# Residual additions of a two-block attention kernel: by VectorE, or by accumulating transfers

## The chip, the core and the metric

The kernel runs on one core of a Trainium2 chip. Its engines are TensorE (PE in the profile; PEld is its weight load), VectorE (DVE), ScalarE (ACT), GpSimd (POOL) and SyncE (SP), which only issues transfers. Each engine executes its own instructions in a fixed order and waits on semaphores for the others. Transfers are issued from an engine's queue and carried out by 16 DMA engines. The metric is device time of one execution in microseconds; lower is better.

## The reference

Eight images of 512 channels by 1024 positions (float32) go through two attention blocks. Cut to what matters:

```python
# layer 0: 32 groups, 8 heads
h = group_norm(x, gn_weight, gn_bias)
q, k, v = split(w_qkv @ h + b_qkv)              # per head, 64 channels
a = softmax(q.T @ k * scale) @ v                # per head
x = x + (w_proj @ a + b_proj)                   # first residual
# layer 1: 8 groups, one head of 512 channels
h = group_norm(x, gamma, beta)
q, k, v = q_w @ h + q_b, k_w @ h + k_b, v_w @ h + v_b
a = softmax(q.T @ k * scale) @ v
return x + (p_w @ a + p_b)                      # second residual
```

The two lines with `x +` are the subject of this study.

## The kernel before

**Tiles.** A channel tile is 128 channels by 1024 positions; an image has four (`KC`). Results are written in halves of 128x512 (`HT` = 512), so that an image has eight half tiles of 256 KB.

**Products.** Matrix products are Strassen–Winograd products. `wino` makes a product of 2x2 blocks with seven block products, taken in the order 1, then a `middle`, then 4 and 3. They accumulate in three kinds of PSUM banks: a (products 1, 2), b (6, 7, 4) and c (5, 3), two of each (i = 0, 1). When a block of the result is complete, `wino` calls `done(i, row, c, ps, u)`, where `ps` is the bank and `u` an intermediate in SBUF (or nothing for the first block). Block (0,0) is complete after product 2, (1,1) after product 7, (1,0) after 4 and (0,1) after 3. The last two products, 4 and 3, are put off (`tail`) and run behind product 1 of the next stage, so that TensorE has work while the other engines empty the banks. `conv2` nests the scheme twice for the convolutions q, k, v and g; some of its additions run on GpSimd (L537), as do the differences that make its inner factors (`inner_factors`, L416).

**Stages.** The loop goes over the images b. Each turn has: layer 0's attention of image b; `projection`, the last convolution of layer 0, of image b; the g convolution and layer 1 of image b-1 (`layer1_scores`, `layer1_rest`); and the v, k and q convolutions of image b+1. So layer 1 of image j ends beside the v convolution of image j+2. While that happens, four "ahead" loads (L209) bring the image after that one, and VectorE takes its statistics (`half_stats`, L98) as background. Image 6's layer 1 has the g convolution of image 7 beside it, and image 7's layer 1 comes at the very end.

**The first residual.** Before the projection, SP loads the four tiles of x (L1062). For each completed block, VectorE adds bank, bias and x into the x tile (L938), then the intermediate u (L942 or L944), and then takes the statistics of the result for layer 1. Its four tiles are stored to a DRAM buffer, `spills[b]`.

**The second residual.** Layer 1 of image b loads `spills[b]` again (`load_again`, L1020). `values1` makes the last product (`av`). For each completed block, VectorE multiplies by the reciprocal sums r into a temporary o (L757, or L759 and L760), adds bias and x into the x tile (L762), and SP stores that half to the output (L763). The factors of this product, `sz`, are sums and differences of z, made by VectorE (L159 to L162) just before and during its first products.

**Order.** A tile scheduler puts the instructions of each engine in an order by priorities and readiness. Only instructions wrapped in `tc.keep_in_program_order` keep the order of the program, all matmuls among them. So TensorE's order is written out by hand, and most of the other engines' order is the scheduler's.

Of the kernel before, what the change touches and what calls it, by code (L numbers as in the profile page):

```python
# [9 lines left out]
F32 = mybir.dt.float32  # L10
I32 = mybir.dt.int32
AF = mybir.ActivationFunctionType
ALU = mybir.AluOpType
# [16 lines left out]
def two_attention_blocks_kernel(  # L30
# [145 lines left out]
    def main_path(ctx):  # L176
# [30 lines left out]
        def load_x(b, c, what):  # L207
            t = big_tile(f"{what}_{b}_{c}")
            nc.sync.dma_start(t, x[b, c * P : (c + 1) * P, :])  # L209
            return t  # L210
# [130 lines left out]
        def weight(n):  # L341
            return weight_factors(weight_part(n))
# [400 lines left out]
            )  # L743
            return total, {p: [x[:, i, :] for x in fs[p] for i in range(2)] for p in fs}

        def values1(b, zf, ef, r, xt, uid, hooks):
            def mm(p, i, ps, start):
                for k in range(4):
                    matmul(
                        ps, zf[p][k // 2][:, k % 2, ts(i, P)], ef[p][k], start=start and k == 0, stop=k == 3, skip_group_check=True  # L750
                    )

            def done(i, row, c, ps, u):
                oc = 2 * row + i
                o = upool.tile([P, HT], F32, tag="o", bufs=2, name=f"o_{uid}_{oc}_{c}")
                if u is None:
                    nc.vector.tensor_mul(o, ps, r[:, c, :])  # L757
                else:
                    nc.vector.tensor_add(o, ps, u)  # L759
                    nc.vector.tensor_mul(o, o, r[:, c, :])  # L760
                xh = xt[oc][:, ts(c, HT)]
                nc.vector.scalar_tensor_tensor(xh, o, obias[1][:, oc : oc + 1], xh, ALU.add, ALU.add)  # L762
                nc.sync.dma_start(out[b, oc * P : (oc + 1) * P, ts(c, HT)], xh)  # L763

            wino(f"av_{uid}", mm, done, middle=(2, 5, 6, 7), hooks=hooks, back=4)
# [125 lines left out]
        def load_again(b, c, what):  # L891
            t = big_tile(f"{what}_{b}_{c}")
            nc.sync.dma_start(t, spills[b][c])
            return t
# [33 lines left out]
        def projection(b, af, xt, hooks=()):  # L928

            norm = GroupNorm(1, f"1_{b}", pinned=b > 0)  # L930
            stats, rest = [], []

            def residual(i, r, c, ps, u):
                oc = 2 * r + i
                xh = xt[oc][:, ts(c, HT)]

                tc.keep_in_program_order(
                    nc.vector.scalar_tensor_tensor(xh, ps, obias[0][:, oc : oc + 1], xh, ALU.add, ALU.add)  # L938
                )
                if (r, c) == (1, 1):  # L940

                    rest.append(lambda: tc.keep_in_program_order(nc.vector.tensor_add(xh, xh, u)))  # L942
                elif u is not None:
                    nc.vector.tensor_add(xh, xh, u)  # L944
                stats.append(lambda: norm.half_stats(oc, c, xh))

                if c == 1 - r:
                    stats.append(lambda: norm.end_stats(oc))

            def add_rest():  # L950
                for f in rest:
                    f()

            def store():
                spills[b] = spool.tile([KC, P, T], F32, tag="spill", name=f"spill_{b}")
                for c in range(KC):
                    nc.sync.dma_start(spills[b][c], xt[c])

            by_channel(
                weight("p"), af, f"p_{b}", residual, middle=(5, 6, 7, 2), hooks=[[], [], hooks, [], [add_rest]],  # L960
                after=[load_weight, store],
            )
            return norm, stats
# [43 lines left out]
        def layer1_rest(b, inner, gf, gsteps, stats, hooks, ahead):  # L1007
            first = query_factors(gf[1], f"1_1_{b}")
            total, ef = scores1(inner, gf, gsteps, first, f"1_{b}", stats)
            state = {}  # L1010

            def sums():
                state["r"] = reciprocals(total, f"1_{b}", True)

            z = by_token(
                weight("z"), hf, f"z1_{b}", hooks=[*hooks, [sums]], back=3,
                after=[load_weight, lambda: background.extend(zsteps)],
            )
            all_background()
            xt = [load_again(b, c, "x") for c in range(KC)]  # L1020
            stiles = [big_tile(f"sz{i}_{b}", (P, 2, 2, C // 2)) for i in (1, 2, 4)]
            halves = lambda t: (t[:, :, : C // 2], t[:, :, C // 2 :])
            zf, zsteps = left_sums(
                [halves(t) for t in z[:2]], [halves(t) for t in z[2:]],
                [lambda j, t=t: t[:, j, :, :] for t in stiles], nc.vector.tensor_add, nc.vector.tensor_sub,
            )
            values1(b, zf, ef, state["r"], xt, f"1_{b}", ahead)

        for b in range(B):
            extra = [[] for _ in range(2 * 2 * KC)]  # L1030
            for i, fs in enumerate(later):
                extra[i] += fs
            later = []
            h, loads, applies = [], [], []
            if b > 0:
                h, loads, applies = begun(load_again, norm1, b - 1, "h1")
            elif B > 1:
                h, loads, applies = begun(load_x, norm0, 1, "h0")
            for f in loads:
                f()  # L1040
            for i, f in enumerate(applies):
                extra[2 * i + 1].append(f)
            a = channel_tiles(f"a0_{b}")

            here = lambda *t: tc.keep_in_program_order(nc.vector.tensor_sub(*t))
            af, steps = image_factors(a, f"a_{b}", here)

            if b > 0:
                hf, t = image_factors(h, f"h1_{b - 1}", here)
                for i, fs in enumerate((t[:1], t[1:2], (t[2], t[4]), (t[6], t[3]), (t[5], t[7]), steps[:2], steps[2:4])):  # L1050
                    extra[2 * i + 3] += fs
            elif B > 1:
                hf, t = image_factors(h, "h0_1", here)
                for i, fs in enumerate((t[:2], (t[2], t[4]), (t[6], t[3]), (t[5], t[7], *steps[:2]), steps[2:4])):
                    extra[2 * i + 7] += fs
            psum_pools(f"attention_{b}", 1)
            scaled = attention0(b, q, k, v, a, extra)
            if B > 1:
                for f in steps[4:7]:
                    f()  # L1060
            psum_pools(f"products_{b}", 2)
            xt = [load_x(b, c, "x") for c in range(KC)]  # L1062
            if B > 1:

                inner, sums2 = inner_factors(hf, f"h1_{b - 1}" if b > 0 else "h0_1", tc.keep_in_program_order)
                for f in sums2:
                    f()
                norm1, stats = projection(b, af, xt, [scaled, steps[7]])
            if b > 0:
                gf, gsteps = layer1_scores(b - 1, inner)  # L1070
                _, _, mean, affine = norm_hooks(norm1, f"1_{b}")
                if b + 1 < B:
                    h, loads, applies = begun(load_x, norm0, b + 1, "h0")
                    ahead, made = factors_ahead(h, loads, applies, f"h0_{b + 1}")
                else:
                    h, loads, applies = begun(load_again, norm1, b, "h1")
                    ahead = [loads, *([f] for f in applies)]
                layer1_rest(b - 1, inner, gf, gsteps, stats, [[], mean, [], affine], ahead)
                if b + 1 < B:
                    v, norm0 = values(b + 1, made["inner"])  # L1080
                    q, k = keys_and_queries(b + 1, made["inner"], norm0, ())
            elif B > 1:
                v, norm0 = values(1, inner)
                hooks = norm_hooks(norm1, "1_0")
                hooks[0].append(lambda: background.extend(stats))
                q, k = keys_and_queries(1, inner, norm0, hooks)
            else:
                for f in (*steps[:7], scaled, steps[7]):
                    f()
                all_background()  # L1090
                norm1, stats = projection(0, af, xt)
                finish()
                background.extend(stats)
                for f in sum(norm_hooks(norm1, "1_0"), []):
                    f()
                h, loads, applies = begun(load_again, norm1, 0, "h1")
                for f in loads + applies:
                    f()
# [202 lines left out]
```

## Time and profile before

| what | value |
| --- | --- |
| median of 3 runs | 2832.25 us (2831.9 to 2833.12) |
| profiled execution | 2831.03 us; its span 2829.2 us, granted clock 0.999 |
| TensorE waiting | about 9 us in all, 3.7 of them for the first weights |
| adds of the first residual, L938 / L942 / L944 | 64 of 0.74 us / 16 of 1.17 us / the rest 0.67 to 1.13 us |
| adds of the second residual, L762 | 64 of 0.75 us |
| x tiles loaded for the first residual / the second | 32 / 32, 512 KB each |
| transfers | q1 (SP) 28.3% of 16 engines' time, q10 (ScalarE) 0.3%; none in a GpSimd queue |
| SP's issue of one transfer, L763 | 0.33 us |

A row of the timeline reads: start in us, duration in us, engine, line, operation, output<-inputs, shape, and in brackets how long the engine had stood idle before it and for whom. Consecutive equal rows may be gathered ("x8"). A row of the waits names the waiting instruction and, behind the arrow, what it waited for.

### The profile page before, as it was taken

To read this page: it belongs to the slowest core of one execution; us is meant where nothing else is said; L and a number is where in the kernel's file an instruction comes from. 1 tells how busy PE (TensorE), PEld (TensorE's weight loads), DVE (VectorE), ACT (ScalarE), POOL (GpSimd) and SP (SyncE) were. 2 spreads that over 40 slices of the span, in tenths; PEclk is the share of its full clock that TensorE was granted. 3 is DMA by queue.
4 is the path that set the end of the run, shared out by engine and by line. 5 is a ranking of instruction groups with operands and counts; after the bars stand their busy time and mean duration, and the time that the engine had idled before them with its cause. 6 is when DMAs were issued, how large, how long until landed. Compare 5 with 4: busy or idle time off the path is not lost.

```text
span 2829.2 us, 33980 instructions
## 1 busy us (share of the span) xinstructions
PE 2811.2 (99%) x12434; PEld 1691.7 (60%) x12434; DVE 2119.0 (75%) x2877; ACT 942.7 (33%) x1205; POOL 1250.6 (44%) x1249
## 2 busy tenths in 40 slices
PE   9999999999999999999999999999999999999998
PEld 5435635866367653677537674376843868338584
DVE  5588687766877778777787667877678776887765
ACT  1252452214522145221552215422154312633130
POOL 2214215842267421674117731277223772147672
PEclk9999999999999999999999999999999999999999
DMA  8634403043031330323212232123311224112301
GB/s 286 210 114 147 151 19 121 26 178 138 20 139 53 146 129 23 131 99 119 110 49 105 101 141 90 49 102 123 139 70 49 102 112 158 35 53 95 119 5 68
DMA packets 98850, 291.68 MB, mean 103 GB/s; under 512 B 10803, under 2 KB 42867, under 8 KB 88950
## 3 DMA queue, kind: packets, MB, share of 16 engines
q1 hardware_dynamic: 96886, 287.16, 28.3%
q10 hardware_dynamic: 1792, 2.29, 0.3%
q8 instruction: 100, 1.64, 0.2%
q14 instruction: 72, 0.59, 0.1%
HBM read 236.94 MB, written 52.47 MB: 102 GB/s over the span
## 4 chain that ended last, share of the span: by engine, by line
PE 97%; DVE 1%; issue 1%; POOL 0%; ACT 0%; DVEq 0%; POOLq 0%
PE sc L67 16%; PE av L67 16%; PE psb_av L67 6%; PE psb L67 5%; PE psa_av L67 4%; PE psc_av L67 4%; PE psc L67 3%; PE psa L67 3%; PE psb_z L67 3%; PE psb_p L67 3%; PE psb_k L67 3%; PE psb_g L67 3%; PE psb_v L67 3%; PE psb_q L67 2%; PE psa_p L67 2%; PE psa_z L67 2%
## 5 line engine op out<-in xcount | busy, mean ns | idle before, releaser
L639 DVE TENSOR_TENSOR sum<-sum,e 128x1024 f32<-128x1024 f32 x384 | 518.9, 1351 | 40.7 <-ACT e L635 0.9
L635 ACT ACTIVATE e<-sc 128x1024 f32<-128x1024 f32 x512 | 476.0, 1054 | 79.1 <-PE sc L67 79.1
L67 PE MATMUL sc<-q,k 64*128 64x512 f32 x2048 | 456.8, 596 | 0.0
L67 PE MATMUL av<-e,v 128*64 128x512 f32 x2048 | 453.6, 595 | 0.0
L67 PEld LDWEIGHTS sc<-q,k 64*128 64x128 f32 x2048 | 191.6, 186 | 238.5 <-ACT e L635 109.2
L67 PEld LDWEIGHTS av<-e,v 128*64 128x64 f32 x2048 | 141.4, 137 | 304.3 <-issue 304.3
L601 POOL TENSOR_TENSOR all_recs<-all_recs,rc 128x256 f32<-128x256 f32 x72 | 63.8, 887 | 541.3 <-DVE rc L599 541.3
L658 POOL TENSOR_TENSOR a<-a,r 128x512 f32<-128x512 f32 x56 | 114.9, 2051 | 261.7 <-DMA r<-rows 245.5
L599 DVE RECIPROCAL rc<-sums 128x256 f32<-128x256 f32 x72 | 126.5, 1756 | 46.7 <-PE sums L67 25.3
L653 ACT COPY a<-av 128x512 f32<-128x512 f32 x64 | 37.4, 585 | 321.9 <-PE av L67 321.9
L637 DVE TENSOR_TENSOR sum<-e,e 128x1024 f32<-128x1024 f32 x64 | 78.8, 1231 | 57.0 <-ACT e L635 57.0
L67 PE MATMUL psb<-inner,inner_h 128*128 128x256 f32 x448 | 116.1, 382 | 0.8
L67 PE MATMUL psa_av<-e,z 128*128 128x512 f32 x256 | 113.3, 595 | 0.0
L416 POOL TENSOR_TENSOR inner_h<-h,inner_h 128x256 f32<-128x256 f32 x120 | 107.5, 897 | 3.4
L140 ACT ACTIVATE h<-h,b,s 128x1024 f32<-128x1024 f32 x62 | 78.5, 1270 | 88.0 <-DMA h<-in_x 70.4
L67 PEld LDWEIGHTS psb<-inner,inner_h 128*128 128x128 f32 x448 | 83.9, 190 | 16.6 <-POOL inner L431 3.5
L464 ACT COPY psb_v<-psa_v 128x512 f32<-128x512 f32 (+1 forms) x28 | 14.5, 517 | 227.0 <-DVE o L759 144.6
L416 POOL TENSOR_TENSOR inner_h<-h 128x256 f32<-128x256 f32 x60 | 55.6, 926 | 77.4 <-ACT h L140 77.4
L699 POOL TENSOR_TENSOR sum<-sum,e 128x1024 f32<-128x1024 f32 x32 | 76.1, 2378 | 27.1 <-ACT e L695 25.9
L67 PE MATMUL psb_g<-inner_h,w_m 128*128 128x256 f32 x336 | 85.9, 383 | 0.3
L685 DVE TENSOR_TENSOR e<-psc,u 128x512 f32<-128x512 f32 x56 | 38.7, 691 | 59.0 <-PE psc L67 58.6
L537 POOL TENSOR_TENSOR v<-v,v 128x256 f32<-128x256 f32 x28 | 20.0, 726 | 141.8 <-DVE u_v L532 141.8
(361 smaller groups left out, 5749.6 us busy)
## 6 DMA issues: line engine op xcount, KB each, us to landing
x<-in_x SPq DMA_DIRECT2D x36, 512.0 KB
h<-in_x SPq DMA_DIRECT2D x32, 512.0 KB
spill<-x SPq DMA_DIRECT2D x32, 512.0 KB
h<-spill SPq DMA_DIRECT2D x32, 512.0 KB
x<-spill SPq DMA_DIRECT2D x32, 512.0 KB
out<-x SPq DMA_DIRECT2D x64, 256.0 KB
w_p<-sums_p SPq DMA_DIRECT2D x8, 1792.0 KB
r<-rows SPq DMA_DIRECT2D x112, 128.0 KB
```

What stands on the lines that cost most here:

```text
L67: tc.keep_in_program_order(nc.tensor.matmul(*args, **kw))
L140: tc.keep_in_program_order(nc.scalar.activation(dst, src, AF.Identity, bias=b, scale=s))
L416: pin(nc.gpsimd.tensor_tensor(dst, x, y, ALU.subtract))
L599: nc.vector.reciprocal(rc, sums)
L601: nc.gpsimd.tensor_tensor(all_recs, all_recs, rc, ALU.add)
L635: nc.scalar.activation(e, sc, AF.Exp, scale=(C // 8) ** -0.5)
L637: nc.vector.tensor_add(total, es[0], e)
L639: nc.vector.tensor_add(total, total, e)
L653: nc.scalar.copy(dst, av)
L658: nc.gpsimd.tensor_tensor(dst, dst, r, ALU.mult)
L685: nc.vector.tensor_add(dst[0], ps, x[0])
L699: on = lambda dst, x, y: lambda: tc.keep_in_program_order(nc.gpsimd.tensor_tensor(dst, x, y, ALU.add))
```

## The change

The result tiles no longer begin as loaded x. The results are written to SBUF with their bias, and then the residual is added to them there by a transfer from DRAM with `accum_op=add`, which reads the tile's half, adds and writes it back. These transfers are issued from GpSimd's queue, one for each half tile of 256 KB.

- First residual, all images: no load of x. Block (0,0) leaves PSUM on ScalarE with the bias; the others leave on VectorE as bank + bias + u in one operation (`biased`). Then the accumulating transfer of x's half follows. The statistics and the store to `spills[b]` come behind it, and so wait for it. The put-off addition of block (1,1) (`add_rest`) is gone.
- Second residual, images 0 to 6: no load from the spill. The multiplied result goes to a tile y, ScalarE adds the bias in place, an accumulating transfer adds the spill's half, and SP stores the half as before. Image 7's layer 1 stays as it was.

In all there are 64 + 56 = 120 accumulating transfers; 32 + 28 loads of 512 KB are gone.

```diff
 def values1(b, zf, ef, r, xt, before, uid, hooks):
     def done(i, row, c, ps, u):
         oc = 2 * row + i
-        o = upool.tile([P, HT], F32, tag="o", ...)
+        if before is None:
+            o = upool.tile([P, HT], F32, tag="o", ...)
+        else:
+            o = xt[oc][:, ts(c, HT)]
         if u is None:
             nc.vector.tensor_mul(o, ps, r[:, c, :])
         else:
             nc.vector.tensor_add(o, ps, u)
             nc.vector.tensor_mul(o, o, r[:, c, :])
+        if before is not None:
+            nc.scalar.activation(o, o, AF.Identity, bias=obias[1][:, oc : oc + 1])
+            nc.gpsimd.dma_start(o, before[oc][:, ts(c, HT)], accum_op=ALU.add)
+            nc.sync.dma_start(out[b, oc * P : (oc + 1) * P, ts(c, HT)], o)
+            return
...
 def projection(b, af, xt, hooks=()):
+    place = biased(xt, obias[0])
     def residual(i, r, c, ps, u):
         oc = 2 * r + i
+        place(i, r, c, ps, u)
         xh = xt[oc][:, ts(c, HT)]
-        tc.keep_in_program_order(
-            nc.vector.scalar_tensor_tensor(xh, ps, obias[0][:, oc : oc + 1], xh, ALU.add, ALU.add)
-        )
-        if (r, c) == (1, 1):
-            rest.append(lambda: tc.keep_in_program_order(nc.vector.tensor_add(xh, xh, u)))
-        elif u is not None:
-            nc.vector.tensor_add(xh, xh, u)
+        nc.gpsimd.dma_start(xh, x[b, oc * P : (oc + 1) * P, ts(c, HT)], accum_op=ALU.add)
         stats.append(lambda: norm.half_stats(oc, c, xh))
...
-    ..., hooks=[[], [], hooks, [], [add_rest]],
+    ..., hooks=[[], [], hooks],
...
 def layer1_rest(...):
-    xt = [load_again(b, c, "x") for c in range(KC)]
+    before = spills[b] if b + 1 < B else None
+    xt = channel_tiles(f"y_{b}") if b + 1 < B else [load_again(b, c, "x") for c in range(KC)]
...
-    values1(b, zf, ef, state["r"], xt, f"1_{b}", ahead)
+    values1(b, zf, ef, state["r"], xt, before, f"1_{b}", ahead)
...
 for b in range(B):
-    xt = [load_x(b, c, "x") for c in range(KC)]
+    xt = channel_tiles(f"x1_{b}")
```

`biased`, which was there already, is the placing function:

```python
def biased(out, bias):
    def done(i, r, c, ps, u):
        oc = 2 * r + i
        dst = out[oc][:, ts(c, HT)]
        if u is None:
            nc.scalar.activation(dst, ps, AF.Identity, bias=bias[:, oc : oc + 1])
        else:
            nc.vector.scalar_tensor_tensor(dst, ps, bias[:, oc : oc + 1], u, ALU.add, ALU.add)
    return done
```

More of the change, by code (lines that the diff above doesn't have):

```diff
@@ L744, in scores1, with values1 @@
             return total, {p: [x[:, i, :] for x in fs[p] for i in range(2)] for p in fs}
-        def values1(b, zf, ef, r, xt, uid, hooks):
+        def values1(b, zf, ef, r, xt, before, uid, hooks):
             def mm(p, i, ps, start):
@@ L754, in done @@
                 oc = 2 * row + i
-                o = upool.tile([P, HT], F32, tag="o", bufs=2, name=f"o_{uid}_{oc}_{c}")
+                if before is None:
+                    o = upool.tile([P, HT], F32, tag="o", bufs=2, name=f"o_{uid}_{oc}_{c}")
+                else:
+                    o = xt[oc][:, ts(c, HT)]
                 if u is None:
@@ L930, in projection @@
             norm = GroupNorm(1, f"1_{b}", pinned=b > 0)
-            stats, rest = [], []
+            stats = []
+            place = biased(xt, obias[0])
             def residual(i, r, c, ps, u):
                 oc = 2 * r + i
+                place(i, r, c, ps, u)
                 xh = xt[oc][:, ts(c, HT)]
-                tc.keep_in_program_order(
-                    nc.vector.scalar_tensor_tensor(xh, ps, obias[0][:, oc : oc + 1], xh, ALU.add, ALU.add)
-                )
-                if (r, c) == (1, 1):
-                    rest.append(lambda: tc.keep_in_program_order(nc.vector.tensor_add(xh, xh, u)))
-                elif u is not None:
-                    nc.vector.tensor_add(xh, xh, u)
+                nc.gpsimd.dma_start(xh, x[b, oc * P : (oc + 1) * P, ts(c, HT)], accum_op=ALU.add)
                 stats.append(lambda: norm.half_stats(oc, c, xh))
@@ L948, in residual @@
                     stats.append(lambda: norm.end_stats(oc))
-            def add_rest():
-                for f in rest:
-                    f()
             def store():
@@ L959, in projection @@
             by_channel(
-                weight("p"), af, f"p_{b}", residual, middle=(5, 6, 7, 2), hooks=[[], [], hooks, [], [add_rest]],
+                weight("p"), af, f"p_{b}", residual, middle=(5, 6, 7, 2), hooks=[[], [], hooks],
                 after=[load_weight, store],
```

## The prediction

> **What bounds the kernel.** First the page: busy shares, the granted clock, the chain that ended last.
>
> ```profile
> span 2829.2 us, 33980 instructions
> PE 2811.2 (99%) x12434; PEld 1691.7 (60%) x12434; DVE 2119.0 (75%) x2877; ACT 942.7 (33%) x1205; POOL 1250.6 (44%) x1249
> PEclk9999999999999999999999999999999999999999
> PE 97%; DVE 1%; issue 1%; POOL 0%; ACT 0%; DVEq 0%; POOLq 0%
> ```
>
> TensorE computes 99% of the span at full clock. Work taken off any other engine is worth only what TensorE waits for it. Next, therefore, TensorE's waits.
>
> ```profile
> PE tr_wk L70 <- DMA rawk<-in_w: 3.7, 1, 3.7
> PE psb_v L67 <- ACT u_v L454: 1.2, 1, 1.2
> PE psa_v L67 <- POOL h L142: 0.8, 1, 0.8
> PE psc_v L67 <- DVE x L938: 0.6, 1, 0.6
> ```
>
> These columns are total, times and longest, in us. With five lines of 0.4 to 0.5 the list sums to about 9 us. The residual's loads (36 + 28 of 512 KB) appear in no line, and the residual's vector work appears only as image 0's 0.6, with 1.2 + 0.5 just behind it. So at most 2.3 us can be gained. What decides is whether the change makes new waits. So the third step is the order of instructions of the built changed kernel, engine by engine, laid on the timeline of before. TensorE's order is the same in both.
>
> **Part 1: removed and moved work.** Per projection VectorE loses 8 operations (16 L938/L942/L944 rows of 0.7 to 1.1 us become 6 adds out of PSUM plus 2 on ScalarE); per layer-1 image 0 to 6 it loses 8 L762 rows of 0.75. That is about 11 us an image of work beside TensorE: nothing for the end, except image 0's 2.3 us at the most. The 60 loads leave SP, which nobody waits for: nothing. ScalarE gains 8 in-place biases (0.72 each, row L544) per layer-1 image, at 33% busy; they are priced where somebody is behind them. New are 120 accumulating transfers of 256 KB in GpSimd's queue. They cost d of GpSimd's time each to issue, and land a time l later; before has no such row. For d the lowest neighbours are SP's own issue (0.33 us, L209) and ScalarE's (0.56); the highest is GpSimd's 128x512 multiply (L658, 2.05). GpSimd's own L128 (a power of 128x4 numbers) takes 1.02 us, nearly all of it without data to move, as an issue is; of these rows it is the nearest in kind. I take d = 1.0. For l: a 512 KB load took 3.6 us from its issue to its first reader (shown below). Half the bytes, but they are read, added and written, so the ends are 2 and 4; I take l = 3.
>
> **Part 2: a sum that slips behind a product.** Image 1's layer 1, VectorE, before, and TensorE below it:
>
> ```profile
> 917.70 0.69 DVE L757 TENSOR_TENSOR o<-psa_av,r 128x512 f32<-128x512 f32 x1 [2.14 <-PE psa_av L67]
> 918.31 0.68 DVE L159 TENSOR_TENSOR sz<-z,z 128x512 f32<-128x512 f32 x1
> ...
> 921.37 0.69 DVE L757 TENSOR_TENSOR o<-psa_av,r 128x512 f32<-128x512 f32 x1
> ```
>
> ```profile
> 917.50 3.60 PE L67 MATMUL psa_av<-e,z 128*128 128x512 f32 x8
> 920.93 3.60 PE L67 MATMUL psc_av<-t,sz 128*128 128x512 f32 x8
> ```
>
> Product 5 (psc_av) multiplies by sz and starts the moment product 2 (psa_av) ends. Both sz sums stand ahead of the second o in before. In the changed order the first operations are y_0, y_1, and only then the two sz: y_1 waits for the end of product 2, so sz can't start sooner. TensorE then waits 0.2 (start after the product's end, as at 917.70) + 0.61 (the pitch of y_1 to the next operation) + 0.68 (first sz) + 0.1 = 1.6 us. The order is alike in all seven changed layer-1 images: 7 x 1.6 = **11.2 us**. This is the surest term.
>
> **Part 3: the statistics ahead are queued behind the new transfers.** While TensorE runs image 1's last products and the next v convolution, the loads "ahead" of a later image are issued by SP and their statistics run on VectorE. Here is before: SP, VectorE, GpSimd and TensorE.
>
> ```profile
> 934.89 5.65 SPq L209 DMA_DIRECT2D ahead<-in_x  x3
> ```
>
> ```profile
> 938.52 0.69 DVE L98 BATCH_NORM_STATS2 bnst<-ahead 128x6 f32<-128x512 f32 x1 [2.96 <-DMA ahead<-in_x]
> ```
>
> ```profile
> 946.33 1.85 POOL L416 TENSOR_TENSOR inner_h<-t_h,inner_h 128x256 f32<-128x256 f32 x2
> 969.86 0.73 POOL L537 TENSOR_TENSOR v<-v,v 128x256 f32<-128x256 f32 x1 [21.68 <-DVE u_v L532]
> ```
>
> ```profile
> 958.15 1.06 PE L67 MATMUL psc_v<-w_v,inner_h 128*128 128x128 f32 x8
> ...
> 965.30 1.06 PE L67 MATMUL psb_v<-w_v,inner_h 128*128 128x128 f32 x8
> ```
>
> The first load's way from issue to reader is 938.52 - 934.89 = 3.6 us. In the changed order SP has the stores of y_2 and y_3 between the loads ahead: ahead_1 stands behind the store of y_3, which waits for its accumulation to land; GpSimd issues that accumulation behind 11 of its L416 operations, and they stand behind y_2's issue, which waits for y_2's bias. The sum, on the clock of before plus the 1.6 of part 2: y_2 biased at 942.8; + d; + 11 x 0.78 = 8.6; + d; + l; store 0.4; load 3.6; two statistics 1.28; then y_0 out of psc_av 0.69. Only then is the bank free that product psc_v wants at 958.15: 957.5 + 2d + l, thus 4.35 us late at d = 1, l = 3. Second link: ahead_3 stands behind the stores of y_2 and y_3's other halves, whose accumulations GpSimd issues 9 operations (7.0) later, two more d: landing at about 963 + 4d + l. Two statistics and two operations of the v convolution (1.28 + 0.67 + 0.76, about 3.0 with the starts) stand before what psb_v wants at 965.30. The delay, part 2 included, is 963 + 4d + l + 3.0 - 965.3 = 0.7 + 4d + l = 7.7 us. Less the 1.6 counted: 6.1 in each of the five images with loads ahead (0 to 4): **30.7 us**. At the lower ends (d = 0.33, l = 2) it is 4.05 - 1.6 = 2.5 each, 12; at the upper ones (2.05, 4) 12.9 - 1.6 = 11.3 each, 57. If GpSimd's operations were not in its way this would be nearly nothing: its idle 21.68 us at 969.86 cover the issues, but not SP's wait and VectorE's.
>
> Image 5 has no load ahead; GpSimd's last issues end near 964.5, before the v additions wanted at 969.86: nothing beyond part 2. Image 6 (beside image 7's g convolution): t_h and ScalarE's h_3 stand behind y_3 on their engines (1.9 us), and the issues precede GpSimd's inner_h and g additions (up to 4 us at d = 1): 7.5 - 1.6 = **5.9 us**; 2.5 to 14 at the ends.
>
> **Part 4: the projections.** Eight accumulations stand on GpSimd between its inner factors and the additions of the g convolution:
>
> ```profile
> 831.01 1.41 POOL L537 TENSOR_TENSOR g<-g,g 128x256 f32<-128x256 f32 x2 [10.73 <-DVE u_g L532]
> ```
>
> The 10.73 us of idle time hide eight issues while d is under 1.34; above it, 8d - 10.7 is lost in each of seven images: 0 at d = 1, 7 x 5.7 = 40 at 2.05. Image 0's projection has no such gap: statistics of the accumulated x stand before v operations that TensorE wants, about +3 against the 2.3 regained, taken as **+1** (0 to 5). The biases of ScalarE and the store of the spill, which now waits for accumulations, stand ahead of weights wanted far later.
>
> **Sum.** 11.2 + 30.7 + 5.9 + 1 = 48.8 us, or 2831.03 + 49 = **2880 us**. The profiled execution lies 1.2 below the median of the runs (2832.25), a small matter here. At the lower ends 11.2 + 12 + 2.5 + 0 = 26 (2857); at the upper ones 11.2 + 57 + 14 + 5 + 40 = 127 (2958).
>
> **A rule against the change.** GpSimd's L416 operation takes 1.17 us beside VectorE's two-input t_h operations (931 to 934 us) and 0.72 when they are over. The Trainium skill, "SBUF — State Buffer", section "SBUF: two separate sides", says that VectorE and GpSimd lock each other out of a shared port, and that a transfer issued by GpSimd then waits, since its descriptors can't be written. By that rule d would be stretched in the same 1.17/0.72, to about 1.6, and the sum, an estimate, would be 11 + 46 + 9 + 3 + 15 = 84. Another page, "DMA: Bandwidth & Descriptors", section "Anatomy of one DMA — SWDGE (gpsimd) path", fits 2.0 us + bytes/436e3 per transfer, 2.6 us for 256 KB; an estimate by it takes 2 us off the sum. No row of before has such a transfer.
>
> **Rivals.** (a) Only part 2 binds: GpSimd takes the issues in its idle time, and the accumulations land early enough. This wants 2d + l under about 2.3 (d = 0.33 and l under 1.6). Then 11 to 14 us: 2843. For it: 21.68 us of idle time in that stage; against: 3.6 us for a load. (b) GpSimd becomes the bound: d above 1.34, so that the projections lose too; 70 to 127 us, 2900 to 2958, with 2930 at d = 1.7. For it: L658's 2.05 and the stretched 1.17; against: a transfer's issue moves no data through the engine. (c) Not slower: VectorE's relief is what counts. Image 0's 2.3 us come back and product 5's wait is hidden, since TensorE's sequencer may have other work there; it decides if the sz sums are done before product 2 ends, as they were in before, and 2d + l is under 2.3. Price: -2.3 to +5, 2829 to 2836. Against: the order on VectorE is fixed, and nothing stands between products 2 and 5. (d) The change doesn't bind as told because the accumulations wait on something else (a slow read, add and write of 8 us or more): beyond 2958.
>
> **Chances.** Forecast (d 0.33 to 1.34) 0.66; (a) 0.10; (b) 0.15; (c) 0.06; (d) 0.03. The range from 2843 to 2945 leaves out (c), (d) and the upper part of (b), under 2 in 10. A measurement of this kernel can tell about 0.2% (5.7 us) from no change. Faster by that needs 5.7 us where TensorE waits for 9 in all, most of it not touched: 0.02. Within it: (c)'s rest, 0.05. Slower 0.93.
>
> **What would show it.** Part 2: seven TensorE waits of about 1.6 us at product 5, psc_av, for VectorE's sz. Part 3: waits of psc_v and psb_v in the v convolutions of images 2 to 6 for VectorE, and VectorE's waits for the loads ahead well above the 3.0 us of before. Part 4: no wait at the g convolutions of images 1 to 7. GpSimd's issue rows give d, the distance to the store gives l. It is wrong if the waits lie in other stages, if d isn't between 0.33 and 1.34, or if the sz waits are missing.

## The result, and the profile after

The changed kernel takes 2913.45 us (median of 4 runs, 2912.89 to 2916.95), before 2832.07: 1.029 times as long, with a 95% interval of 1.0277 to 1.0303, about 81 us more. The profiled execution took 2916.95 us, its span 2915.2, so that the two profiles lie 86 us apart. Four lines of the page of after, in the order of its parts (span, busy time, queues, chain):

```profile
span 2915.2 us, 34074 instructions
PE 2832.9 (97%) x12434; PEld 1708.7 (59%) x12434; DVE 2098.7 (72%) x2757; ACT 988.9 (34%) x1277; POOL 1310.2 (45%) x1369
q0 software_dynamic: 17280, 31.46, 6.7%
PE 89%; DVE 5%; DMA 2%; POOL 2%; issue 1%; ACT 0%; SPq 0%; DVEq 0%; POOLq 0%; ACTq 0%
```

The new queue q0 carries the 120 accumulations (31.46 MB). VectorE lost 20 us of busy time, less than intended: with layer 1's transfers left out (below) it loses 93 (2119.0 to 2026.1 us), and the difference lies in the long operations shown further down. The kernel gained none of it. The chain that ended last now passes through VectorE, GpSimd and transfers. TensorE, with the same 12,434 products, is busy 21.7 us longer and idle 64.3 us longer (2915.2 - 2832.9 against 2829.2 - 2811.2). Its waits (total, times, longest):

```profile
PE psc_v L67 <- DVE y L762: 31.9, 6, 6.3
PE psb_v L67 <- DVE u_v L532: 13.4, 7, 3.1
PE psc_av L67 <- DVE sz L159: 10.8, 7, 1.5
...
PE psa_g L67 <- DVE t_h L170: 1.7, 1, 1.7
PE psb_g L67 <- ACT u_g L454: 1.3, 1, 1.3
PE psb_g L67 <- POOL inner_h L416: 1.1, 1, 1.1
```

The third line is part 2 of the prediction, seven times 1.5 us. The first is a wait in six stages, one more than the prediction had: 5.6 to 6.3 us each in those of images 0 to 4, and 3.1 in image 5's.

TensorE's order is the same in both kernels, so every product can be matched with itself, and the difference of its starts read off along the run. It grows only here:

| where | growth, us | forecast |
| --- | --- | --- |
| image 0's projection and the v convolution behind it | 3.8 | 1 |
| product 5 in seven layer-1 stages | 12.5 (7 x 1.8) | 11.2 |
| rest of the stages of images 0 to 4 | 13.2, 10.7, 10.6, 10.7, 11.4 | 6.1 each |
| rest of image 5's stage | 6.2 | 0 |
| rest of image 6's stage | 6.6 | 5.9 |
| projections of images 1 to 7 | 0 | 0 |

What happens in image 1's stage is on VectorE's timeline, here in part:

```profile
964.32 7.33 DVE L763 TENSOR_TENSOR y<-y,r 128x512 f32<-128x512 f32 x1
...
973.37 6.99 DVE L763 TENSOR_TENSOR y<-y,r 128x512 f32<-128x512 f32 x1
...
984.80 0.68 DVE L762 TENSOR_TENSOR y<-psc_av,u_av 128x512 f32<-128x512 f32 x1
```

A multiply that takes 0.69 us elsewhere takes 7.33 and 6.99. It isn't waiting for a semaphore: it has begun, and doesn't end. GpSimd at the same time:

```profile
962.69 0.89 POOL L766 DMA_DIRECT2D y<-spill  x1 [9.30 <-ACT y L765]
963.31 1.03 POOL L416 TENSOR_TENSOR inner_h<-h 128x256 f32<-128x256 f32 x1
...
970.14 0.95 POOL L416 TENSOR_TENSOR inner_h<-h,inner_h 128x256 f32<-128x256 f32 x1
972.76 0.89 POOL L766 DMA_DIRECT2D y<-spill  x1 [1.68 <-ACT y L765]
```

An issue, and at once a run of 11 L416 operations, each starting before the one ahead has ended (0.68 from start to start, 1.03 to 0.95 long). VectorE's multiply ends at 971.65, when the run is over. Then ScalarE adds the bias, GpSimd issues the next accumulation at 972.76, a second run follows, and the next multiply stands still until 980.36. Behind it are the statistics and the operation at 984.80, which frees the bank that TensorE wants:

```profile
985.53 2.08 PE L67 MATMUL psc_v<-w_v,inner_h 128*128 128x128 f32 x8 [6.29 <-DVE y L762]
988.02 2.08 PE L67 MATMUL psb_v<-w_v,inner_h 128*128 128x128 f32 x8 [0.41 <-ACT u_v L454]
```

Eight products that took 1.06 us before take 2.08 here. The table by stretches says why; its columns are the stretch, its length, busy time and instructions of PE, PEld, DVE, ACT and POOL, the granted clock, the DMA engines' busy share and GB/s:

```profile
975.00:980.00 5.00, 4.24 (x22) 2.70 (x20) 5.00 (x1) 0.00 (x0) 4.81 (x8) 1.00 0.36 92
980.00:985.00 5.00, 0.00 (x0) 0.00 (x0) 4.37 (x9) 1.44 (x2) 1.76 (x2) 0.71 0.94 259
985.00:990.00 5.00, 4.05 (x17) 3.76 (x18) 3.80 (x8) 2.29 (x5) 0.95 (x2) 0.50 0.69 158
990.00:1000.00 10.00, 9.34 (x73) 9.15 (x73) 5.69 (x13) 2.10 (x5) 0.79 (x1) 0.89 0.64 160
```

During the wait the granted clock falls to half, and it stays there some microseconds after the work is back. The trace has such a stretch in the six stages of images 0 to 5 and nowhere else before the end, 47.6 us in all; 47.6 us at half clock can stretch TensorE's work by up to 23.8, and its busy time rose by 21.7.

Image 6's stage, which has a g convolution beside it, has one long row too: a t_h difference that begins 0.1 us into a run of 13 L416 operations behind an issue, and lasts over the whole run. The waits of 1.1, 1.0 and 1.3 us for inner_h, a bank and u_g (the list above) come behind it.

```profile
2754.34 9.60 DVE L173 TENSOR_TENSOR t_h<-h,t_h 128x512 f32<-128x512 f32 x1
```

### The profile page after: what moved, and what is told of

It reads as the page before. It is cut to its first block, busy times and chain, and to the rows that moved or that the text cites. A ratio compares the mean times of both kernels' runs of the same rounds, so it can differ in the third digit from the quotient of the medians.

```text
span 2915.2 us, 34074 instructions
## 1 busy us (share of the span) xinstructions
PE 2832.9 (97%) x12434; PEld 1708.7 (59%) x12434; DVE 2098.7 (72%) x2757; ACT 988.9 (34%) x1277; POOL 1310.2 (45%) x1369
## 3 DMA queue, kind: packets, MB, share of 16 engines
q0 software_dynamic: 17280, 31.46, 6.7%
## 4 chain that ended last, share of the span: by engine, by line
PE 89%; DVE 5%; DMA 2%; POOL 2%; issue 1%; ACT 0%; SPq 0%; DVEq 0%; POOLq 0%; ACTq 0%
PE sc L67 15%; PE av L67 15%; PE psb L67 5%; PE psb_av L67 4%; PE psa_av L67 4%; PE psc L67 3%; PE psa L67 3%; PE psb_z L67 3%; PE psb_k L67 3%; PE psb_g L67 2%; PE psb_p L67 2%; PE psb_q L67 2%; PE psc_av L67 2%; DVE y L763 2%; PE psa_z L67 2%; PE psb_v L67 2%
## 5 line engine op out<-in xcount | busy, mean ns | idle before, releaser
L765 ACT ACTIVATE y<-y,obias 128x512 f32<-128x512 f32 x56 | 40.4, 722 | 332.6 <-DVE y L763 239.7
L766 POOL DMA_DIRECT2D y<-spill x56 | 49.5, 911 | 210.9 <-ACT y L765 206.4
L416 POOL TENSOR_TENSOR inner_h<-h,inner_h 128x256 f32<-128x256 f32 x120 | 109.5, 913 | 3.0
L763 DVE TENSOR_TENSOR y<-y,r 128x512 f32<-128x512 f32 x42 | 108.7, 2589 | 0.9
L67 PE MATMUL psb_v<-w_v,inner_h 128*128 128x128 f32 x588 | 84.5, 293 | 17.9 <-DVE u_v L532 13.4
L67 PEld LDWEIGHTS psb_v<-w_v,inner_h 128*128 128x128 f32 x588 | 77.1, 204 | 25.2 <-DVE u_v L532 14.2
```

Source lines behind the costliest of these rows:

```text
L67: tc.keep_in_program_order(nc.tensor.matmul(*args, **kw))
L416: pin(nc.gpsimd.tensor_tensor(dst, x, y, ALU.subtract))
L765: nc.scalar.activation(o, o, AF.Identity, bias=obias[1][:, oc : oc + 1])
L766: nc.gpsimd.dma_start(o, before[oc][:, ts(c, HT)], accum_op=ALU.add)
```

## The experiments

Three causes stood against one another for the stages' loss. The **queue theory** is the record's: loads ahead wait on SP behind stores that wait for accumulations. The **lock theory** came from the rows above: a GpSimd run directly behind an issue shuts VectorE out of some operations until the run ends. The third was that the accumulation's own traffic holds VectorE up.

| kernel | median, us | ratio to before, 95% interval |
| --- | --- | --- |
| changed kernel | 2913.45 | 1.0277 to 1.0303 |
| first residual only | 2836.32 | 1.0006 to 1.0025 |
| second residual only | 2910.62 | 1.0265 to 1.0300 |
| second residual's transfers left out | 2848.00 | 1.0038 to 1.0072 |
| sz first | 2897.51 | 1.0217 to 1.0251 |
| multiply from PSUM | 2888.42 | 1.0186 to 1.0220 |
| plain store by GpSimd | 2857.96 | 1.0077 to 1.0111 |
| sz first and multiply from PSUM | 2874.48 | 1.0138 to 1.0171 |
| no two-operand VectorE work beside the runs | 2922.24 | 1.0298 to 1.0333 |
| stores left out | 2901.06 | 1.0224 to 1.0258 |
| all cures | 2854.58 | 1.0060 to 1.0093 |

**The two engines by themselves.** A kernel of its own with nothing but this:

```python
issue()                                  # none, plain, or accumulating, on GpSimd
for i in range(11): gpsimd.tensor_tensor(gb[i % 2], ga[:, 256:], ga[:, :256], subtract)
for i in range(3):  vector.tensor_mul(vo, va or a PSUM bank, vb)
```

> Leaves the whole computation out: it only sets GpSimd and VectorE side by side, 4 times 8 sections. In a section GpSimd runs 11 subtractions of 128x256 from SBUF, VectorE three multiplies of 128x512; VectorE's first begins about 1 us into the run. Ahead of GpSimd's run stands nothing, a plain transfer, an accumulating one, or an accumulating one and then a wait of some 2 us for ScalarE; VectorE multiplies two tiles of SBUF, or a PSUM bank by a tile. Lock theory (a run of GpSimd directly behind an issue shuts VectorE's two-input operations out until the run ends): the first two-input multiply takes 5 to 7 us behind either kind of transfer, 0.7 to 1.3 us where no transfer or a wait stands ahead; the multiply from PSUM takes 0.7 everywhere. Rival (the long rows of the changed kernel come from the accumulation's traffic in SBUF): long rows behind the accumulating transfer alone, with PSUM too. Queue theory: no row over 1.3 us anywhere.

VectorE's rows behind an accumulating issue, first with two tiles of SBUF, then from PSUM:

```profile
54.25 10.17 DVE L72 TENSOR_TENSOR vo<-va,vb 128x512 f32<-128x512 f32 x3
...
67.23 2.14 DVE L74 TENSOR_TENSOR vo<-vps,vb 128x512 f32<-128x512 f32 x3
```

Of the 10.17 us the first multiply took 8.72. It took 8.71 to 8.72 in all four rounds behind an accumulating issue, 8.42 to 8.43 in three of four behind a plain one (1.14 in the other), and 0.86 to 1.25 without an issue. From PSUM it took 0.69 each time, with the accumulation under way. So traffic is out, and the lock theory stands for either kind of transfer. The sections with a wait said nothing: VectorE had finished before GpSimd's run began.

**Where the shut-out ends.** The same with runs of 4, 11 and 20, other operations of VectorE, and waits of GpSimd for ScalarE at two places.

> Leaves the whole computation out; as the first measurement of the two engines side by side, 4 times 8 sections, now for where the shut-out ends and for which operations. Behind an accumulating issue GpSimd runs 4, 11 or 20 subtractions while VectorE wants a two-input multiply of 128x512: lock theory expects 3, 8 to 9 and 14 to 15 us, the end of the run each time; if it were a fixed time of the transfer, the same in all three. Statistics of one tile (one operand in SBUF): 0.7. A copy from SBUF to SBUF: unknown, 0.7 or the whole run. With a wait of GpSimd for ScalarE between issue and run: 0.9 to 1.3, the two taking turns, if running on without a gap is what shuts VectorE out; 8 if it is the issue as such. With such a wait behind the fourth subtraction: 3 to 4, the multiply getting in at the gap. The copy without an issue: the value to hold the other against.

First round, in order: 11 and 20 subtractions, statistics, copy, wait ahead of the run, wait behind the fourth subtraction, copy without an issue (two operations a row).

```profile
15.79 9.43 DVE L76 TENSOR_TENSOR vo<-va,vb 128x512 f32<-128x512 f32 x2
...
28.76 15.48 DVE L76 TENSOR_TENSOR vo<-va,vb 128x512 f32<-128x512 f32 x2
...
47.71 1.41 DVE L78 BATCH_NORM_STATS2 st<-va 128x6 f32<-128x512 f32 x2
...
58.69 8.88 DVE L80 COPY vo<-va 128x512 f32<-128x512 f32 x2
...
72.94 1.99 DVE L76 TENSOR_TENSOR vo<-va,vb 128x512 f32<-128x512 f32 x2
...
84.38 5.10 DVE L76 TENSOR_TENSOR vo<-va,vb 128x512 f32<-128x512 f32 x2
...
96.21 1.45 DVE L80 COPY vo<-va 128x512 f32<-128x512 f32 x2
```

The first operation of each took 8.71, 14.76, 0.68, 8.42, 0.86, 3.97 and 0.59 us, and the other rounds agree within 0.03 us; the run of 4 held it 3.96 us in three rounds of four, 1.05 in the first. The shut-out lasts to the first gap in GpSimd's work, whatever the transfer does; a wait that makes such a gap ends it. It strikes a multiply of two SBUF tiles and a copy from SBUF to SBUF, not the statistics and not the multiply that reads PSUM.

An issue ahead isn't needed for it. In the kernel before, where GpSimd issues no transfer, the multiplies by r in the layer 1 of images 0 and 3 fell into a run of L416 and were held over four operations, to the next gap in that run:

```profile
596.02 3.34 DVE L760 TENSOR_TENSOR o<-o,r 128x512 f32<-128x512 f32 x1
...
1633.21 3.41 DVE L760 TENSOR_TENSOR o<-o,r 128x512 f32<-128x512 f32 x1
```

Nor is it always enough: the plain issue of the first round (1.14 us) and the second run behind an issue in each stage of the plain store below didn't bring it. So the lock theory's "directly behind an issue" tells where the long rows of the changed kernel stand, not what starts them.

The Trainium skill, "SBUF — State Buffer", section "SBUF: two separate sides", names the same operations: VectorE with two SBUF inputs or in its fast copy mode shares a port with GpSimd as an exclusive lock. It gives the lock to one instruction at a time and warns that VectorE then holds up GpSimd's issue. The runs agree on the operations, and differ on the length: GpSimd kept VectorE out over 11 and 20 instructions. The warning, which is about the fast copy mode, isn't tested: no run sets such a copy ahead of an issue. Beside the two-operand work of layer 1 an issue took 0.88 us in the median, as alone.

**The two residuals apart.** Each half of the change with the other as before.

```diff
-            before = spills[b] if b + 1 < B else None
-            xt = channel_tiles(f"y_{b}") if b + 1 < B else [load_again(b, c, "x") for c in range(KC)]
+            before = None
+            xt = [load_again(b, c, "x") for c in range(KC)]
```

> The first residual as changed, the second as before. Both theories: nothing in the projections of images 1 to 7 (the changed kernel's trace has no new wait there), image 0 about 3.5 us: 2835 to 2837. If the issues of the first residual disturb the layer-1 stages as well: over 2845.

> The second residual as changed, the first as before. Prediction on record: 11.2 + 30.7 + 5.9 = +48, 2880. By the changed kernel's trace, stage by stage: +78, 2908 to 2912, with VectorE rows of 7 us twice a stage.

As by the trace: 2836.32 and 2910.62. By the matched starts the first residual costs 3.2 us in image 0 and nothing in the seven other projections (the medians lie 4.8 apart); the second makes the rest.

**Transfers left out.** GpSimd issues nothing for layer 1.

```diff
-                    nc.gpsimd.dma_start(o, before[oc][:, ts(c, HT)], accum_op=ALU.add)
```

> The changed kernel without the second residual's transfers (images 0 to 6 lack that addition); y, bias and stores stay. Queue theory and lock theory alike: no store waits for a landing, GpSimd issues nothing, so what is left is the sz slip of seven stages (12.6 by the trace) and image 0 (3.5): 2846 to 2850. If the 7 us rows come from the order of VectorE and GpSimd alone and not from the issue: they stay, and the time is over 2885.

2848.00, and the longest y multiply is 1.26 us. Matched product by product, the slips are still 12.5 us, image 0 has 3.0, image 6's stage 1.8, and the six other stages 0.4 or less either way. No multiply was shut out. So everything beyond 2848 hangs on the transfers of layer 1, by their issue or by their landing.

**sz first.** The program issues the two sz sums ahead of product 2's results.

```diff
-                after=[load_weight, lambda: background.extend(zsteps)],
+                after=[load_weight, lambda: [f() for f in zsteps[:2]], lambda: background.extend(zsteps[2:])],
```

> The changed kernel with the two first sz sums issued by the program ahead of product 2's results; every other engine's order stays. If the slip of part 2 costs what the trace says (7 x 1.8), 2913.5 falls to 2900 or 2902, and the seven waits of psc_av for sz are gone. If VectorE's later rows absorb it: within 3 of 2913.

2897.51: 15.9 less, some 3 more than expected, and none of the seven waits is left. The matched starts give 12.5 of it to the slips; the rest is spread over the stages.

**Multiply from PSUM.** Bank + u goes to a spare bank, and the multiply by r reads it there.

```diff
-                    nc.vector.tensor_add(o, ps, u)
-                    nc.vector.tensor_mul(o, o, r[:, c, :])
+                    s = acc_tile(f"s_{uid}_{oc}_{c}")
+                    nc.vector.tensor_add(s, ps, u)
+                    nc.vector.tensor_mul(o, s, r[:, c, :])
```

> The changed kernel, but bank + u goes to a spare PSUM bank and the multiply by r reads it there, so that it has one operand in SBUF; the accumulations and the stores' waits stay (GpSimd's issue of y_3 moves four operations forward). Lock theory alone (the 7 us rows are the cause): no row over 1.3 us at the multiply, the stages of images 0 to 5 lose nearly nothing beyond the sz slip: 2847 to 2855. Queue theory of the record (SP's stores ahead of the loads ahead are the cause): the stages still lose 4 to 8 us each: 2870 to 2890, with VectorE waiting 4 us or more for loads ahead.

2888.42, with the widest spread here (2883.91 to 2894.44). All 42 multiplies took 0.69 us or less, but the lock found the next operation of its kind, a t_h difference:

```profile
960.92 0.68 DVE L764 TENSOR_TENSOR y<-s,r 128x512 f32<-128x512 f32 x1
961.52 6.93 DVE L173 TENSOR_TENSOR t_h<-h,t_h 128x512 f32<-128x512 f32 x1
```

Image 5's stage, without loads ahead, lost 0.5 us in place of 6.2; the five others still 6.2 to 9.6, and there VectorE waits for a load ahead (3.54 us for one in image 1's stage). The test didn't take the lock away as meant, and the stages point to both causes.

**Plain store by GpSimd.** The issue stays, SP has nothing to wait for.

```diff
-                    nc.gpsimd.dma_start(o, before[oc][:, ts(c, HT)], accum_op=ALU.add)
-                    nc.sync.dma_start(out[b, oc * P : (oc + 1) * P, ts(c, HT)], o)
+                    nc.gpsimd.dma_start(out[b, oc * P : (oc + 1) * P, ts(c, HT)], o)
```

> The changed kernel with GpSimd issuing the plain store of y to the output at the very place of the accumulation, and no store on SP (images 0 to 6 lack the second residual). GpSimd's and VectorE's orders are those of the changed kernel; nothing on SP waits for a landing. Queue theory: 2846 to 2852, as without the transfer. Lock theory (any issue will do): the 7 us rows stay, psc_v waits as before: 2885 to 2905.

2857.96, between the two. A plain issue took 0.55 us, not 0.88, and only one multiply in each of the stages of images 0 to 5 was shut out (7.04 us in image 1's); the other took 1.26 there. The stages of images 0 to 4 lost 1.9 to 2.2 us each, so that one shut-out alone, with SP free, is nearly covered. Since the second one vanished with the shorter issue, this run doesn't decide. Image 6's stage had no long row and lost 1.8.

**Stores left out.** Accumulations, issues and the orders of GpSimd and VectorE stay; nothing on SP waits for a landing.

```diff
-                    nc.sync.dma_start(out[b, oc * P : (oc + 1) * P, ts(c, HT)], o)
```

> The changed kernel without the stores of y (images 0 to 6 aren't written out). GpSimd's issues, their accumulation and the orders of GpSimd and VectorE stay; no load ahead waits for a landing. Queue theory alone: 2846 to 2852. Lock theory alone: two rows of 7 us a stage stay, and 8 to 11 us a stage with them: 2895 to 2912. If the two add up: in between, and this less 2848 plus e8 less 2848 gives about the 65 us that the changed kernel loses beyond 2848.

2901.06, and 12 multiplies of 7 us, two a stage in the stages of images 0 to 5:

```profile
L763 DVE TENSOR_TENSOR y<-y,r x42: 665/692/7340, 600.2 to 2756.4; 128x512 f32<-128x512 f32 x42
```

(least, median, greatest in ns). The stages lose 8.0, 9.0, 8.3, 8.1, 7.7 and 6.0 us. Image 6's stage lost 6.6, against 1.8 with the transfers left out, and its t_h difference took 9.61. VectorE waits for no load ahead here (19.2 us in the changed kernel, 15.1 in the one before). So with the loads ahead free, the shut-outs and what follows from them, half clock included, cost 2901.06 - 2848.00 = 53 us: 47 in the six stages, 5 in image 6's. The stores add 2913.45 - 2901.06 = 12, which is the queue's share if their traffic costs nothing of its own.

**No two-operand work beside the runs.** Multiply from PSUM, and the t_h differences ahead of GpSimd's runs.

```diff
-                hooks[3] += [*applies[2:], inner[1], *t[2:4]]
-                hooks[4] += [*inner[2:4], lambda: background.extend([*t[4:6], *inner[4:6], *t[6:], inner[6]])]
+                hooks[3] += [*applies[2:], inner[1], *t[2:4], *t[6:]]
+                hooks[4] += [*inner[2:4], lambda: background.extend([*t[4:6], *inner[4:7]])]
```

> The changed kernel with the multiply from PSUM, and VectorE's two t_h differences (L173) made ahead of the stretch in which GpSimd works off L416, so that nothing with two operands in SBUF is left there on VectorE. The stores still wait for the accumulations, and SP's order still mixes them with the loads ahead. No row of 7 us is expected on VectorE. Queue theory: 4 to 8 us a stage stay in the five stages with loads ahead: 2868 to 2888. Lock theory: 2848 to 2855.

2922.24, slower than any other and beyond both expectations, with no VectorE row of 7 us left in the stages of images 0 to 5 (in image 6's an h difference, L172, took 9.62). Image 5's stage loses nothing (-0.1), the five with loads ahead 13.8 to 14.6 us each. VectorE and TensorE in image 1's stage:

```profile
989.16 0.69 DVE L98 BATCH_NORM_STATS2 bnst<-ahead 128x6 f32<-128x512 f32 x1 [8.01 <-DMA ahead<-in_x]
```

```profile
993.65 1.22 PE L67 MATMUL psc_v<-w_v,h 128*128 128x128 f32 x4 [9.77 <-ACT c_v L454]
```

This is the queue chain of the prediction in pure form. The scheduler had moved two loads ahead on SP behind a store (of y_2's other half), whose accumulation GpSimd issued at 978.82, behind a run; SP issued the load at 983.05, and it had landed at 989.16. So the chain is real and can cost more than the prediction gave it. But SP's and VectorE's orders differ from the changed kernel's, so the run doesn't say how much it costs there, and the sum of the last expectation doesn't come out: 53 and 74 (2922.24 - 2848.00) against 65.

**Cures together.** First sz and the multiply from PSUM; then also the early differences, with the stores of images 0 to 4 put behind the loads ahead (`pending.append(store)`, flushed there).

> The sz sums first and the multiply from PSUM together. Lock theory: 2835 to 2842. Queue theory: 2858 to 2877. Neither expects it below before, since TensorE waited for nothing that the change removes.

> All cures together: sz sums first, the multiply from PSUM, the early t_h differences, and the stores of images 0 to 4 put behind the loads ahead in the program. What is left is image 0 (3.5) and image 6's stage (2 to 5): 2836 to 2845 by both theories; if GpSimd's time for 120 issues costs something of its own, more.

2874.48 for the first, 14 us under the multiply from PSUM alone. That is in the range of the queue theory, but a t_h difference of 6.9 us was shut out in each of the six stages there too, so it doesn't decide. With all of them 2854.58, still 22 us over before and 10 over what was expected: stages of images 0 to 4 lose 2.7 to 3.7 us, image 6's 5.3 (with an h difference of 9.60), image 0 has 2.0. TensorE's longest list is now

```profile
PE psc_v L67 <- ACT c_v L454: 8.3, 5, 1.7
PE psb_v L67 <- ACT u_v L454: 6.2, 5, 1.9
```

ScalarE's copies for the v convolution stand near the y biases on that engine; whether the biases are the cause was not tried. No version beat the kernel before.

## Why the prediction was right, and where it was not

The sign, and a time inside the range (2880, 2843 to 2945), were right; the forecast of +49 was too small by 32, and the largest term had the wrong main cause.

- **That nothing is gained:** right. Without the transfers of layer 1 the kernel keeps VectorE's relief and loses the loads, and is 16 us slower, not faster.
- **Part 2, 11.2 us:** right in place and mechanism. 12.5 by the matched starts, seven waits of 1.5, gone with sz first.
- **Part 3, 6.1 us a stage for the queue:** this step failed. The stages lost 10.6 to 13.2 us. The lock, which the prediction didn't have, makes 8.2 of a stage (stores left out, mean of images 0 to 4). The queue adds 2.5 (by the medians) to 3.1 (by the profiles, where the changed kernel's is the slowest of its four runs), half of the forecast or less, though the no-two-operand run shows that it can cost 14 in another order. The two aren't summed: a late multiply and a late load delay the same operations. Image 5's 6.2 us, forecast at nothing, are lock alone: 6.0 with the stores left out, -0.1 and 0.5 where the multiply read PSUM. Waits in a stage that the prediction left out were also one of its own signs of being wrong.
- **The rule weighed against the change** named the right two engines and was read the wrong way round. The prediction let VectorE stretch GpSimd's issue; d was 0.88 us, 1.0 assumed, not the 1.6 of that estimate. It was GpSimd that shut VectorE out. The estimate's sum isn't right either: at d = 1.6 the formula of part 3 gives about 43, not 46.
- **Clock:** not in the prediction, which took a wait of TensorE at its length. The stretches at half clock come on top, within the losses of the stages: of the 86 us between the profiles, 21.7 are a longer busy time and 64.3 idle time.
- **Landing:** 4.3 us (median of layer 1) where l = 3 was taken. This line is from the groups of after:

```profile
DMA to landing us min/median/max: 3.6/4.3/7.0
```

- **Part 4, projections:** right. Eight issues took 7.12 us together, and GpSimd still stood idle 5.94 us before the g additions. This refutes rival (b).

```profile
837.31 7.12 POOL L946 DMA_DIRECT2D x<-in_x  x8
850.37 1.41 POOL L537 TENSOR_TENSOR g<-g,g 128x256 f32<-128x256 f32 x2 [5.94 <-DVE u_g L532]
```

- **Image 0, +1:** mis-sized; 3.8 (3.2 in the first residual alone). The 2.3 us came back as forecast, and then 6.1 were lost where 3 were taken. Eight accumulations in a row landed 8.3 us after their issue in the median of all projections, 12.0 at most, more than the sum had let them take.
- **Image 6, 5.9:** 6.6, so near by luck. Its t_h part is 1.8 (transfers left out), as told. The other 4.8 were put down to GpSimd's time for the issues, but they come behind the 9.60 us shut-out: in the plain store, where GpSimd still issues eight transfers and no row is long, nothing is lost beyond the 1.8.
- **Rivals (a), (c), (d):** (a)'s 11 to 14 us is nearly what is left (16) when layer 1's transfers are left out, so that the transfers are what it overlooked; of (c)'s relief image 0's 2.3 us showed, but product 5's wait wasn't hidden; in (d) the accumulations were to land after 8 us or more, and layer 1's took 4.3. Rival (b)'s time at d = 1.7 comes to some 2920 by the prediction's own terms, not 2930.

## What to carry to other kernels

Before work is moved to GpSimd's queue, look at what GpSimd computes right behind the issue and which VectorE operations with two SBUF operands fall into that run: they can be held until the run's first gap, and the profile shows it as one long operation, counted as busy, not as a wait. Read a moved result's new place in every engine's order, and ask what a store that now waits for a landing holds up behind it. Where one engine is busy 99%, work taken from the others buys nothing, and new waits are the only thing that can happen to the time.

## What the hardware showed that was not expected

- The shut-out: 3.96, 8.7 and 14.8 us behind an issue for runs of 4, 11 and 20 GpSimd subtractions, against 0.86 to 1.25 without an issue; but 3.34 and 3.41 in the kernel before, without one. What decides whether GpSimd's run keeps VectorE out or takes turns with it stays open. That its operations start before the one ahead has ended doesn't tell: alone with VectorE they did so by 0.04 us without an issue, by 0.03 to 0.06 behind a plain one and by 0.2 to 0.4 behind an accumulating one.
- Alone, an accumulating issue of 256 KB took GpSimd 0.88 us and landed after 3.7, a plain one 0.58 and 2.9 (medians). The estimate of 2.6 us by the Trainium skill, "DMA: Bandwidth & Descriptors", section "Anatomy of one DMA — SWDGE (gpsimd) path", is near the plain one; the accumulating one is above it.
- In each of the six stages with a wait of psc_v of 3.1 to 6.3 us the granted clock was at half for 6.8 to 10.2 us, and eight products took 2.08 us in place of 1.06. With all cures, where no such wait passed 2 us, the v convolutions of these stages had no such stretch. The length of one wait doesn't decide alone: image 0's of 3.1 us brought none. Laid out in slots of 3.41 us, the shortest stretch in this trace, half clock began behind slots in which TensorE stood idle for 2.2 us or more; after the first 20 us no other slot had more than 1.7.
